# Two-layer graph network with mixture of experts: edge work re-paced, all first-layer output products ahead of the table, table's zeros moved up

## The chip, the cores and the metric

The kernel runs on one core of a Trainium2 chip. The metric is device time in microseconds (us), lower is better: the median of 3 runs of the kernel before is 2243.9 us (2240.32 to 2245.11).

## The reference, cut to what matters

625 nodes with 1024 features, 10,000 edges. Layer 0 adds a graph attention and a linear attention to x, then a feed-forward block with ternary weights; layer 1 follows with a mean over neighbours, another linear attention, and experts. The change touches layer 0 and the start of layer 1:

```python
xn = _layernorm(x)
# graph attention (4 heads of 64)
h = rmsnorm(xn) @ W_down;  xl = h @ Wl;  xr = h @ Wr
e = (leaky_relu(xl[src] + xr[dst]) * att).sum per head
alpha = segment_softmax(e, dst);  gat = segment_sum(alpha * xl[src], dst) @ W_up
# linear attention (16 heads)
q, k = elu(xn @ W + b) + 1;  v = xn @ W_v + b_v
kv = k^T v per head;  mix = (q kv / (q sum(k) + eps)) @ W_o + b_o
x = x + gat + mix
x = x + ffn(_layernorm(x))        # weights rounded to -1, 0, 1 by their mean size
xn = _layernorm(x)                # layer 1: k and v products of its attention come first
```

Self loops are added to the edges. The softmax needs no order of edges: scores are exponentiated and written into a dense table by (source, destination), and repeated edges are handled by a matrix of counts.

## The kernel before, in words

Nodes are in 5 tiles of 125 rows. Five engines work side by side, each in program order: TensorE (products), VectorE and ScalarE (elementwise), GpSimd (indirect transfers), SyncE (SP; weight loads). Inside layer 0 the order on each engine is the order in which the Python code emits instructions.

**Stream.** `do(prep, pe, after, after2)` emits the products `pe` of one step; its `after` (evictions by VectorE and ScalarE) is emitted at the next call of `do`, `after2` at the one after that. So an eviction stands on VectorE behind whatever was emitted for the step in between.

**Edge stage (L378 to L723).** The 10,000 edges are 79 chunks of 128 (the last of 16), two chunks to a group, 40 groups. For a chunk GpSimd gathers the rows xl[src] and xr[dst] (L588, two indirect transfers); VectorE adds them, applies `att` and sums to scores (L596, L568, L569, L571); ScalarE exponentiates (L575); GpSimd scatters the scores into a table of 128 × 3080 rows of 4 in DRAM (L602). The table is filled with zeros first (L554, one 6.16 MB transfer of SP, put behind the first loads of Wk, Wv and their biases). The tiles `ga`, `gb` have 4 buffers each.

Meanwhile TensorE does layer 0's linear attention: for each of two halves of the features, 5 key and 5 value pieces (L241, L261: 8 products of 512 columns each), after each of which 6 chunks of edges are counted (L436: 5 products each from one-hot rows that VectorE makes); then the states kv; then 8 queries and answers (L302, L322), in which VectorE takes reciprocals (L333); then the output products `mixed(t)` (L691: for each half of the output 8 products of 512 columns). `mixed(0)` is begun in this stage, the other tiles' come later.

**What paces the edges.** Each piece of TensorE calls `work(us)` with a cost written in by hand: 6.9 for a key or value, 0.7 for a counted chunk, 3.0 for a state, 8.5 for a query, 3.5 for an answer. Whenever these units pass the next multiple of 7.6, one beat is emitted (L642): scores of group g−2, exponentials of group g−3, and for each of the two chunks two gathers of group g and one scatter of group g−3. In beats 1 to 5 the self loops of a tile are added (L618). Beats that are left over are emitted after the last step (L720).

**After the table (L725 to L1038).** `load_table(t)` reads the block of one tile of destinations back (L760, GpSimd's queue); x is loaded again on the same queue (L972). Here too the absolute sums of the three feed-forward weights are taken (L736), their mean is made by a small product (L740), and the weights are rounded (L751). `weigh(t)` multiplies the table's block by the counts (L774, VectorE). The loop over p (L992 to L1034) then does for tile p `sums` (pg, L797), `turn_sums`, and `up_again` (L829), whose product is accumulated into the same PSUM tile as `mixed(p)`; and for tile p−1 the feed-forward block (f1 to f4), for tile p−2 the second normalisation (p5, f5). Biases `bo` are added to x at L1020, two tiles in each of p = 0, 1 and the last in p = 2. Two slots in each turn of p hold a `spacer` (L982): one half of `mixed(p+2)` while p+2 < 5, and from p = 3 on a key or value piece of layer 1; what is left of those follows the loop (L1035). Layer 1's weights are loaded at p = 3 (L995).

Of the kernel before, what the change touches and what calls it, by code (L numbers as in the profile page):

```python
# [53 lines left out]
def attempt(ctx: ExitStack, tc: tile.TileContext, w: dict, out: bass.AP, shifted: bool):  # L54
# [161 lines left out]
    class LinearAttention:  # L216
# [13 lines left out]
        def half(self, c):  # L230
            Wk, bk, Wv, bv = (w[n] for n in self.names[1:])
            self.wk, self.wv = Half(wpool, Wk, c), Half(wpool, Wv, c)
            self.bk, self.bv = self.bias(bk, c, "bk_t"), self.bias(bv, c, "bv_t")
            self.kf = mid([P, NT, 512], "kf")
            self.v = mid([P, NT, 4, 129], "v")
            nc.gpsimd.memset(self.v[:, :, :, 128:129], 1.0)
            self.kv.append(mix.tile([128, 4, 256], FP, tag="kv", name="kv", bufs=2))

        def key(self, t):
# [19 lines left out]
            self.work(6.9)  # L259

        def value(self, t):  # L261
# [12 lines left out]
            self.work(6.9)  # L274

        def states(self):
# [5 lines left out]
            def state(a):  # L282
# [15 lines left out]
                self.work(3.0)  # L298
# [3 lines left out]
        def query(self, m):  # L302
# [17 lines left out]
            self.work(8.5)  # L320

        def answer(self, m, oT):  # L322
# [14 lines left out]
            self.work(3.5)  # L337

    with ExitStack() as st0:
# [8 lines left out]
        with ExitStack() as edges:  # L348
# [31 lines left out]
            nc.gpsimd.memset(none, FAR if shifted else 0.0)  # L380
            sf = pool.tile([128, EN], FP, name="sf")
# [153 lines left out]
            for t in range(NT):  # L535
# [9 lines left out]
                if t == NT - 2:  # L545
# [8 lines left out]
            nc.sync.dma_start(out=table.rearrange("(p a b) h -> p a (b h)", p=128, a=28),  # L554
                              in_=none.unsqueeze(1).to_broadcast([128, 28, 440]))

# [25 lines left out]
            def gather(g, j):  # L582
                lo, n, p = groups[g]
                if j == 0:
                    ab[g] = [pool.tile([128, G, 256], FP, tag=k, name=k, bufs=4) for k in ("ga", "gb")]
                if j < n:
                    for dst, src, ix in ((ab[g][0], xl_d, si), (ab[g][1], xr_d, di)):
                        nc.gpsimd.indirect_dma_start(  # L588
                            out=dst[0:p, j, :], out_offset=None, in_=src[:, :],
                            in_offset=bass.IndirectOffsetOnAxis(ap=ix[0:p, lo + j:lo + j + 1], axis=0))  # L590
# [8 lines left out]
            def scatter(g, j):  # L599
                lo, n, p = groups[g]  # L600
                if j < n:
# [38 lines left out]
            beat = dict(us=0.0, g=0)  # L640

            def work(us):  # L642
                beat["us"] += us
                while beat["us"] >= 7.6 * beat["g"] and beat["g"] < len(groups) + 3:
                    g = beat["g"]
                    beat["g"] += 1
                    if 1 <= g <= NT:
                        self_loops(g - 1)
                    if g >= 3:
                        lo, n, p = groups[g - 3]  # L650
                        exp(es[0:p, lo:lo + n, :])
                    if 2 <= g < len(groups) + 2:
                        score_group(g - 2)
                    for j in range(G):
                        if g < len(groups):
                            gather(g, j)
                        if g >= 3:
                            scatter(g - 3, j)
# [3 lines left out]
            for c in range(2):  # L662
                if c:
                    lin.half(c)
                for t in range(NT):
                    for f in (lin.key, lin.value):
                        f(t)
                        part["held"] = max(part["held"] - 1, 0)
                        for _ in range(6):
                            if count():  # L670
                                work(0.7)
# [19 lines left out]
            def mixed(t, ks=range(KC)):  # L691
                for c in range(2):
                    def pe(c=c):
                        if c == 0 and ks[0] == 0:
                            hold["px", t] = ps2("px1")
                        for k in ks:
                            nc.tensor.matmul(hold["px", t][:P, c, :], lhsT=oT[:, k, nodes(t)], rhs=wo[c](k),  # L697
                                             start=(k == 0), stop=False)

                    yield lambda pe=pe: do(None, pe)  # L700

            for m in range(KC):
                if m + 1 < KC:
                    lin.query(m + 1)
                else:
                    for f in mixed(0, range(6)):
                        f()
# [10 lines left out]
            bo = [lin.bias(w["L0_bo"], c, tag) for c, tag in enumerate(("bk_t", "bv_t"))]  # L718
            do.flush()
            while beat["g"] < len(groups) + 3:  # L720
                work(8.0)
# [6 lines left out]

        gu = wpool.tile([128, KC, 512], BF, tag="w", name="gu", padded_shape=[128, KC, 512])
        dn = late.tile([128, 2, D], BF, name="dn")  # L730
        made = [gu[:, :, 0:256], gu[:, :, 256:512], dn]
        part3 = late.tile([128, 3], FP, name="part3")
        wmean = late.tile([128, 3], FP, name="wmean")
        wscale = late.tile([128, 3], FP, name="wscale")

        def weight_sums():  # L736
            for i in range(3):
                nc.vector.tensor_reduce(part3[:, i:i + 1], raw[i], AX.X, ALU.add, apply_absolute_value=True)

        def weight_means():  # L740
            def pe():
                hold["pm"] = ps1("pm")
                group(hold["pm"][:, 0:3], [(ones, part3)])

            def after():
                nc.vector.tensor_scalar(wmean, hold["pm"][:, 0:3], 1.0 / (256 * D), 1e-5, op0=ALU.mult, op1=ALU.max)
                nc.vector.reciprocal(wscale, wmean)

            do(None, pe, after)

        def ternary(i):  # L751
            v = raw[i]
            nc.vector.tensor_scalar(v, v, wscale[:, i:i + 1], 1.0, op0=ALU.mult, op1=ALU.min)
            nc.vector.tensor_scalar(v, v, -1.0, MAGIC, op0=ALU.max, op1=ALU.add)
            m = made[i]
            nc.vector.tensor_scalar(m, v.rearrange("p (k n) -> p k n", k=m.shape[1]), MAGIC, None,
                                    op0=ALU.subtract)
# [71 lines left out]
        def up_again(t):  # L829
            px = hold.pop(("px", t))  # L830
# [1067 lines left out]
```

## Time and profile before

| what | value |
|---|---|
| median of 3 runs | 2243.9 us |
| profiled execution: its own time | 2243.64 us |
| profiled execution: span | 2241.8 us |
| TensorE busy | 2126.3 us (95%) |
| VectorE / ScalarE / GpSimd busy | 713.6 / 194.7 / 347.6 us |
| TensorE busy, 150 to 200 us, granted clock | 35.5 of 50 us, 0.85 |
| TensorE busy, 250 to 300 us, granted clock | 35.4 of 50 us, 0.86 |
| TensorE busy, 300 to 350 us, granted clock | 39.8 of 50 us, 0.89 |
| TensorE busy, 550 to 600 us, granted clock | 40.6 of 50 us, 0.90 |
| TensorE busy, 650 to 700 us, granted clock | 50.0 of 50 us, 1.00 |

The span is that of the instructions on the chip; the execution's own time lies 1.84 us above it. "Busy" counts an engine's instructions only; a waiting engine is idle. A product in 32-bit floats appears as two matrix instructions in the profile, so a piece of 8 products is listed as x16. The granted clock is TensorE's rate as a share of full speed. In a timeline each row has start, duration, engine, line, operation, output and inputs, how many, and in brackets the idle time before it with what ended it.

### The profile page before, as it was taken

The numbers are of one execution on the slowest core, as the hardware profiler recorded it, in microseconds if no ns is written. First come the engines' busy times: TensorE is split into PE (matmuls) and PEld (weight loads), VectorE is DVE, ScalarE is ACT, GpSimd is POOL, SyncE is SP. The second block draws the span as 40 slices with busy tenths as digits, with TensorE's granted clock in tenths as the row PEclk, the third lists the DMA queues.
The fourth block names the chain that finished last, engine by engine and source line by source line (L and its number), as shares of the span: only waits on it lengthen the run. The fifth ranks groups of instructions, "written<-read, shape, count | busy, mean of one in ns | idle before, by whom it ended". The sixth has DMA issues, their size and how long they took to land. (4 is left out here: it accounts for less than half of the span.)

```text
span 2241.8 us, 17353 instructions
## 1 busy us (share of the span) xinstructions
PE 2126.3 (95%) x6934; PEld 1217.0 (54%) x6934; DVE 713.6 (32%) x1212; ACT 194.7 (9%) x354; POOL 347.6 (16%) x351
## 2 busy tenths in 40 slices
PE   7988788898899989999999999999999999999998
PEld 6655365454444657764445767556754444444443
DVE  4864556766421580000113124322111111111112
ACT  2100011011110210000000111110000000000000
POOL 1676767300000040010000000110000000000010
PEclk9999899998899999999999999999999999999999
DMA  9334253421122110231212111030198997898742
GB/s 286 114 108 136 67 175 102 113 83 47 38 85 75 41 54 1 75 141 38 75 38 103 38 38 38 19 103 29 65 334 320 332 330 279 325 332 296 267 148 93
DMA packets 145849, 301.63 MB, mean 135 GB/s; under 512 B 12370, under 2 KB 22436, under 8 KB 145754
## 3 DMA queue, kind: packets, MB, share of 16 engines
q1 hardware_dynamic: 123412, 243.18, 30.5%
q0 software_dynamic: 17664, 47.47, 7.1%
q10 hardware_dynamic: 4678, 9.72, 1.4%
q8 instruction: 58, 0.95, 0.2%
q14 instruction: 37, 0.30, 0.0%
HBM read 277.49 MB, written 22.84 MB: 134 GB/s over the span
## 5 line engine op out<-in xcount | busy, mean ns | idle before, releaser
L130 PE MATMUL pu<-w,xgT 128*128 128x512 f32 x768 | 333.9, 593 | 1.9 <-DVE xgT L1192 1.9
L130 PEld LDWEIGHTS pu<-w,xgT 128*128 128x128 f32 x768 | 144.0, 190 | 174.8 <-issue 172.0
L130 PE MATMUL pyb<-w,hb 128*128 128x512 f32 x384 | 174.3, 598 | 2.4 <-ACT yb L105 2.1
L130 PE MATMUL pq<-xnT,w 128*128 128x313 f32 x512 | 144.1, 441 | 16.1 <-DVE v L269 14.6
L130 PE MATMUL pk<-w,xnT 128*125 128x512 f32 x320 | 141.0, 593 | 4.7 <-DVE x L940 4.7
L130 PE MATMUL pv<-w,xnT 128*125 128x512 f32 x320 | 140.7, 592 | 1.2 <-ACT xnT L956 1.2
L130 PE MATMUL p<-tT,w 128*128 128x313 f32 x512 | 136.3, 428 | 0.4 <-DVE tT L1192 0.4
L130 PEld LDWEIGHTS pq<-xnT,w 128*128 128x128 f32 x512 | 100.3, 197 | 59.3 <-DVE v L269 15.4
L130 PEld LDWEIGHTS pyb<-w,hb 128*128 128x128 f32 x384 | 69.8, 189 | 90.9 <-issue 74.8
L130 PEld LDWEIGHTS p<-tT,w 128*128 128x128 f32 x512 | 96.8, 190 | 37.9 <-issue 1.2
L1732 DVE TENSOR_TENSOR su<-pu,su 128x512 f32<-128x512 f32 x24 | 16.6, 692 | 314.6 <-ACT su L1731 314.6
L130 PEld LDWEIGHTS pk<-w,xnT 128*125 128x125 f32 x320 | 59.4, 188 | 78.1 <-issue 71.2
L130 PEld LDWEIGHTS pv<-w,xnT 128*125 128x125 f32 x320 | 59.7, 188 | 73.3 <-issue 71.6
L1715 POOL DMA_INDIRECT xg<-rows_d,slots x12 | 11.4, 949 | 524.7 <-PE pxg L1722 448.9
L602 POOL DMA_INDIRECT table<-es,at x79 | 82.7, 1047 | 56.6 <-issue 25.5
L588 POOL DMA_INDIRECT ga<-xl_d,si x79 | 81.7, 1034 | 32.5 <-issue 21.7
L588 POOL DMA_INDIRECT gb<-xr_d,di x79 | 82.3, 1042 | 24.1 <-issue 23.8
L697 PE MATMUL px<-w,oT 128*125 128x512 f32 x160 | 75.0, 625 | 6.3 <-DVE oT L334 4.6
L130 PE MATMUL px<-w,hT 128*125 128x512 f32 x160 | 70.3, 592 | 0.0
L130 PE MATMUL px<-w,oT 128*125 128x512 f32 x160 | 70.3, 592 | 0.0
L130 PE MATMUL ph<-meanT,w 128*128 128x313 f32 x256 | 70.1, 426 | 0.0
L130 PE MATMUL ph<-xnT,w 128*128 128x313 f32 x256 | 70.0, 427 | 0.0
(365 smaller groups left out, 2476.5 us busy)
## 6 DMA issues: line engine op xcount, KB each, us to landing
w<-in_eW_dram SPq DMA_DIRECT2D x144, 1024.0 KB
w<-in_L_Wk_dram SPq DMA_DIRECT2D x8, 1024.0 KB
w<-in_L_Wv_dram SPq DMA_DIRECT2D x8, 1024.0 KB
w<-in_L_Wq_dram SPq DMA_DIRECT2D x8, 1024.0 KB
w<-in_L_Wo_dram SPq DMA_DIRECT2D x8, 1024.0 KB
w<-in_W_self_dram SPq DMA_DIRECT2D x8, 1024.0 KB
w<-in_W_neigh_dram SPq DMA_DIRECT2D x8, 1024.0 KB
w<-in_sW_dram SPq DMA_DIRECT2D x8, 1024.0 KB
```

Source lines behind the costliest of these rows:

```text
L130: nc.tensor.matmul(dst, lhsT=lhsT, rhs=rhs, start=(i == 0), stop=(i == len(pairs) - 1))
L588: nc.gpsimd.indirect_dma_start(out=dst[0:p, j, :], out_offset=None, in_=src[:, :], in_offset=bass.IndirectOffsetOnAxis(ap=ix[0:p, lo + j:l ...
L602: nc.gpsimd.indirect_dma_start(out=table[:, :], out_offset=bass.IndirectOffsetOnAxis(ap=at[0:p, lo + j:lo + j + 1], axis=0), in_=es[0:p, l ...
L697: nc.tensor.matmul(hold["px", t][:P, c, :], lhsT=oT[:, k, nodes(t)], rhs=wo[c](k), start=(k == 0), stop=False)
L1715: nc.gpsimd.indirect_dma_start(out=xg, out_offset=None, in_=rows_d[:, :], in_offset=bass.IndirectOffsetOnAxis(ap=slots[:, b:b + 1], axis=0))
L1732: nc.vector.tensor_tensor(su, pu[:, 0, :], su, op=ALU.mult)
```

## The change

- *Pacing.* The units become 4.8 for a key or value, 0.72 for a counted chunk, 0.6 for a state, 8.6 for a query, 2.7 for an answer, 0.6 per product of `mixed`; a beat is 8.2 units. Scores lag 3 groups, exponentials 4, scatters 5; from the output products on, 1, 1 and 2. Scatters are taken from one list of chunks, up to two in a beat, up to four in a beat with short lags.
- *Output products.* All five tiles' `mixed` are emitted in the edge stage. The PSUM tiles of 0, 1 and 2 stay as before; those of 3 and 4 are evicted with the bias added into an SBUF tile `kept`, and are added to x in place of the bias. `up_again` for these two starts a new PSUM tile. The weight sums, means and rounding move into the edge stage as well, between the output products.
- *Loop.* No spacers at p = 0 and 1; one (the second) at p = 2; both from p = 3 on. All spacers are key and value pieces of layer 1. The biases of tiles 0 and 1 are added at p = 0, the rest at p = 1. Layer 1's first weights are loaded at p = 0. The second `load_table` stands behind all loads of x.
- *Zeros.* The 6.16 MB transfer is issued right behind the loads of x, W_down, Wl and Wr.

```diff
-            self.work(6.9)
+            self.work(4.8)
-                self.work(3.0)
+                self.work(0.6)
-            self.work(8.5)
+            self.work(8.6)
-            self.work(3.5)
+            self.work(2.7)
...
             nc.gpsimd.memset(none, FAR if shifted else 0.0)
+            nc.sync.dma_start(out=table.rearrange("(p a b) h -> p a (b h)", p=128, a=28),
+                              in_=none.unsqueeze(1).to_broadcast([128, 28, 440]))
...
             lin.half(0)
-            nc.sync.dma_start(out=table.rearrange("(p a b) h -> p a (b h)", p=128, a=28),
-                              in_=none.unsqueeze(1).to_broadcast([128, 28, 440]))
...
+            chunks = [(g, j) for g, (lo, n, p) in enumerate(groups) for j in range(n)]
+            def scatter(last):
+                if chunks and chunks[0][0] <= last:
+                    g, j = chunks.pop(0)
...
+            lags = [3, 4, 5]
+            def one_beat():
+                g = beat["g"]
+                beat["g"] += 1
+                if 1 <= g <= NT:
+                    self_loops(g - 1)
+                if lags[1] > lags[0]:
+                    raise_all(g - lags[1])
+                    scores(g - lags[0])
+                else:
+                    scores(g - lags[0])
+                    raise_all(g - lags[1])
+                for j in range(G):
+                    if g < len(groups):
+                        gather(g, j, 0)
+                        if lags[1] == lags[0]:
+                            scatter(g - lags[2])
+                        gather(g, j, 1)
+                    scatter(g - lags[2])
             def work(us):
                 beat["us"] += us
-                while beat["us"] >= 7.6 * beat["g"] and beat["g"] < len(groups) + 3:
...
+                while beat["us"] >= 8.2 * beat["g"] and chunks:
+                    one_beat()
...
-                                work(0.7)
+                                work(0.72)
...
+            lags[:] = 1, 1, 2
+            kept = mid([P, 2, 2, 512], "kept")
+            mixed(3, keep=kept[:, 0])
+            weight_sums()
+            mixed(4, keep=kept[:, 1])
+            weight_means()
+            mixed(0, range(6, KC))
+            for t in (1, 2):
+                mixed(t)
+                ternary(t)
+            ternary(0)
             do.flush()
-            while beat["g"] < len(groups) + 3:
-                work(8.0)
+            while chunks:
+                one_beat()
...
         load_table(0)
-        weight_sums()
-        for f in mixed(0, range(6, KC)):
-            f()
-        weight_means()
-        do()
-        for i in range(3):
-            ternary(i)
         for t in range(NT):
             rows_dma(nc.gpsimd, x[:, t, :], xrows[t])
-            if t == 0:
-                load_table(1)
-        first_mixed = list(mixed(1))
-        first_mixed[0]()
+        load_table(1)
         weigh(0)
-        first_mixed[1]()
...
-        def spacer(p, c):
-            if p + 2 < NT:
-                if c == 0:
-                    made_of["mixed"] = list(mixed(p + 2))
-                made_of["mixed"][c]()
-            else:
-                f, t = next(kv_pieces)
-                getattr(lin1, f)(t)
+        def spacer():
+            f, t = next(kv_pieces)
+            getattr(lin1, f)(t)
         for p in range(NT + 2):
             do()
-            if p == NT - 2:
-                lin1.half(0)
...
-            spacer(p, 0)
+            if p >= 3:
+                spacer()
...
-            for t in range(2 * p, min(2 * p + 2, NT)):
+            for t in ((0, 1), (2, 3, 4))[p] if p < 2 else ():
                 for c in range(2):
                     xc = x[:, t, c * 512:(c + 1) * 512]
-                    nc.vector.tensor_tensor(xc, xc, bo[c][:P], op=ALU.add)
-            if p <= NT:
-                spacer(p, 1)
+                    nc.vector.tensor_tensor(xc, xc, bo[c][:P] if t < 3 else kept[:, t - 3, c, :], op=ALU.add)
+            if p == 0:
+                lin1.weights(0)
+            if p == 1:
+                lin1.half(0, loaded=True)
+            if 2 <= p <= NT:
+                spacer()
```

`scores(last)` and `raise_all(last)` emit the scores and exponentials of all groups up to `last` that are not emitted yet.

## Prediction

> **What bounds the kernel now.** I read the page first: over the 2241.8 us span TensorE is busy 2126 us, and the slices that are not full lie in the first third.
>
> ```profile
> PE   7988788898899989999999999999999999999998
> PEclk9999899998899999999999999999999999999999
> ```
>
> Each digit is 56 us; the diff touches only slices up to about 650 us. From 624 us on the timeline shows TensorE without a gap for a long way, so a change is worth what it moves that point. Next the waits of TensorE and VectorE before 850 us (total us, times, longest):
>
> ```profile
> PE po L130 <- DVE oT L334: 18.6, 11, 3.7
> PE pq L130 <- DVE v L269: 14.6, 1, 14.6
> PE pkv L130 <- DVE v L269: 8.8, 1, 8.8
> DVE ga L596 <- DMA gb<-xr_d,di: 105.6, 27, 8.4
> ```
>
> TensorE waits for VectorE, and VectorE sits with a score at its head (L596) that waits for a gather. So GpSimd's edge transfers are behind. Its timeline (start, us) says why they end when they do:
>
> ```profile
> 59.83 1.27 POOL L588 DMA_INDIRECT ga<-xl_d,si  x1 [8.41 <-DMA table<-none]
> 203.95 1.00 POOL L602 DMA_INDIRECT table<-es,at  x1 [0.30 <-issue]
> 268.79 1.00 POOL L602 DMA_INDIRECT table<-es,at  x1 [0.30 <-issue]
> 393.39 1.47 POOL L602 DMA_INDIRECT table<-es,at  x1 [2.85 <-DMA table<-es,at]
> 396.26 0.97 POOL L602 DMA_INDIRECT table<-es,at  x1 [1.40 <-DMA table<-es,at]
> 399.13 0.96 POOL L602 DMA_INDIRECT table<-es,at  x1 [1.91 <-DMA table<-es,at]
> 410.81 0.85 POOL L602 DMA_INDIRECT table<-es,at  x1 [1.91 <-issue]
> 413.43 0.90 POOL L164 DMA_DIRECT2D tb<-table  x1 [1.76 <-DMA table<-es,at]
> ```
>
> From 59.8 us GpSimd issues nearly back to back: between the rows at 203.95 and 268.79 lie 48 transfers, 1.35 us each. There are 237 (79 chunks, three each), some 322 us of issuing. The last scatters, with no gathers between, come 2.87 us apart. The table is read from 413.43. Then the handover, on TensorE and VectorE:
>
> ```profile
> 419.47 19.28 PE L697 MATMUL px<-w,oT 128*125 128x512 f32 x43
> 428.14 4.91 DVE L774 TENSOR_TENSOR pT<-tb,CT 125x500 f32<-125x500 f32 x5
> 438.59 4.48 PE L130 MATMUL pg<-xl,pT 125*125 125x65 f32 x40
> 455.67 1.29 DVE L857 BATCH_NORM_STATS2 st<-x 125x6 f32<-125x512 f32 x2
> 485.02 1.27 DVE L857 BATCH_NORM_STATS2 st<-x 125x6 f32<-125x512 f32 x2
> 513.94 1.28 DVE L857 BATCH_NORM_STATS2 st<-x 125x6 f32<-125x512 f32 x2
> 524.72 8.66 PE L130 MATMUL pg<-xl,pT 125*125 125x65 f32 x40 [0.93 <-ACT xnT L956]
> 552.18 1.27 DVE L857 BATCH_NORM_STATS2 st<-x 125x6 f32<-125x512 f32 x2
> ```
>
> While the table is on its way TensorE does output products (L697); its first sum (pg) starts at 438.59. The statistics of one node tile after another (L857) then come 29.4, 28.9 and 38.2 us apart. That is the loop's period, a chain through VectorE and TensorE.
>
> [...] the 40 pg products take 4.48 us in a busy stretch and 8.66 us at 524.72 after short gaps. [...] here a scatter lands 2.1 us after its issue, and a scatter waits for the scatter before it. [...]
>
> **The change, part by part.** All against the profiled execution (span 2241.8, its own time 2243.64, 0.26 under the median of 2243.9). A difference of 0.2%, 4.5 us, is about what a measurement tells from no change.
>
> *A, zeros.* They (6.16 MB) move in SP's queue from behind to ahead of the first key and value weights (4 MB) and two biases. In the built order of the changed program the first half of Wk also waits for the semaphore lane that the zeros use. The loads ahead are some 4.1 MB, moved by about 19.5 us (132 to 284 GB/s in the 5 us stretches); the zeros at about 340 GB/s take 18.5 more, landing near 40; [...] Wk at about 46, and TensorE asks for it at 48.14. Behind that wait on SP stand the other three halves and both biases; they follow 3 us apart, and TensorE and VectorE ask for them later than that. Cost +1 (0 to +5). The first gather may start a few us before 59.83: worth nothing, since from now the pacing holds GpSimd.
>
> *B, when the table is done.* A key or value piece takes TensorE 6.87 us (timeline, 69.87 to 76.74) but now counts 4.8; six counts take 4.00 us for 4.32. A beat of 8.2 thus takes 10.87 × 8.2 / 9.12 = 9.8 us, and without counts 6.87 × 8.2 / 4.8 = 11.7. Before it was 7.6 / 11.1 × 10.87 = 7.4 us, under the 8.2 that GpSimd needs for six transfers, hence the stalls. Now VectorE waits less and GpSimd idles. With four gather buffers a gather waits for the score four groups back, one beat earlier. Without stalls query 0 starts at 48.1 + 20 × 6.87 + 79 × 0.667 + 4 × 1.12 = 242.7, when 155.3 units have passed: beats 0 to 18, beat 19 with that query. GpSimd has then issued 80 gathers and, scatters starting at beat 5, 30 scatters by about 246: 110, where before had 129. The other 127 × 1.36 = 172.7 bring it to 418.9. Added: 4 because in the query part scores stand behind VectorE's 5.7 us of reciprocal and its neighbours; 2 for the catching-up beats, in which scatters alternate with single gathers (2.72 us against the 2.87 that one needs); 4.5 for the last three scatters; 1.8 to the read. So the read is at 431.2 instead of 413.4: +17.8 (+10 to +25; high if the 4 MB of next weights, now loaded as soon as the output products are done, slow scatters as the stalls at 297 to 312 suggest).
>
> The stalls removed from TensorE (8.8, 14.6, most of 18.6, half clock after them) don't count: TensorE is done near 404 and waits for the table.
>
> *C, handover.* Before, 438.59 − 413.43 = 25.2 us. The ternary weights (L753 to L756, 11.3 us) and output products that stood in it are now done ahead of it. Left: 0.9 second issue, 7.5 landing, 4.9 weighing, 0.2: 13.5. −11.7.
>
> *D, tile 0.* TensorE has been idle some 35 us: pg takes up to 8.7 instead of 4.5. The four bias adds stay. Before, 17.0 from pg to x; now 8.7 + 0.8 + 0.8 + 7 (up product at half rate) + 1.2 = 18.5 to 19.5. +2 (0 to +4).
>
> *E, tile 1.* Two product pieces (13.7 us) leave, but VectorE's chain remains: statistics to xq 6.7, transposes to hidden 7.7, weighing 4.95, bias adds (now six) 3.6, tail 4: about 28 with waits, before 29.4. −1 (−4 to +1).
>
> *F, tile 2.* Two product pieces leave, one key comes, in the second slot. That is the row of tile 3 (38.2) without its first slot (pg starts 5.8 earlier), but with a key where it had a value: its bias add (0.7) and its Exp and Relu on ScalarE (1.36 us, VectorE's wait between L248 and L256) now stand ahead of the copy of goT that the up product waits for, so that product starts some 3.5 after the piece instead of 1.1 (544.64 to 545.76): +2.4. 34.8 against 28.9: +6 (−4 to +8).
>
> *G, tiles 3 to 5.* Keys and values change slots: +2.4, and −1.1 for pg's wait behind the same ScalarE work at 524.72 and 562.97 (0.93 and 1.15), each; the last without an up product. +3 (−2 to +6).
>
> *H.* One key or value piece fewer is left after the loop: −6.9.
>
> Free: four evictions of kept tiles (4 × 0.69) and 6.7 us of weight sums on VectorE, hidden under 13.7 us product pieces with no eviction of their own; uncovered they would cost 9.5. The second table read, now behind ten loads of x on GpSimd's queue (0.5 to 1.3 each), lands near 450, and the weighing that needs it comes after the half-rate pg, near 454; were pg at full rate, up to 2 of D would go there.
>
> Sum: 1 + 17.8 − 11.7 + 2 − 1 + 6 + 3 − 6.9 = +10.2, so 2254.
>
> **Rivals.** *The loop was held by TensorE (faster).* Place: tiles 1 and 2. For: in 462.66 to 491.76 TensorE is busy 27.4 of 29.1 us, VectorE 20.4. Then the removed pieces shorten tiles 1 and 2 by 4 each and the slot exchange costs nothing: E and F −4, G 0: 1 + 17.8 − 11.7 + 2 − 8 − 6.9 = −5.8, 2238. It decides once the distance of the statistics in tile 2 falls under 25 us. Against: most of VectorE's other 8.7 us are waits inside the chain itself, for products that wait for VectorE.
>
> *Transfers collide (slower still).* A at +5 and B at +25: 2265. For: GpSimd's stalls at 297 to 312 fall on weight loads issued from 292.5.
>
> *It cancels.* B at +11 with F near zero: 2240 to 2248. For: before also had some 10 us of scatter stalls that might not recur.
>
> **How the numbers follow.** Forecast 0.52 at 2254 (2249 to 2262); TensorE-held loop 0.17 at 2238; collisions 0.17 at 2265; cancelling 0.14. Faster 0.17, same 0.14, slower 0.69. The range 2236 to 2266 leaves about half of the first and third rival's cases out.
>
> **What would show it.** Right: TensorE without waits over 2 us from 48 to 400, then idle some 35 us; first table read near 431; sums at half clock; L857's successor about 28, then 35 us apart. Wrong: the table read before 420; TensorE waiting for Wk at 48; tile 2 under 29 us; or waits inside the edge stage that I count as gone.

## The result and the profile after

The changed kernel takes 2252.94 us (median of 13 runs, 2248.77 to 2262.26), the kernel before beside it 2240.59 us (13 runs, 2237.92 to 2245.11): a ratio of 1.0052, 95% interval 1.0042 to 1.0062, so some 12 us slower. The profiled execution has a span of 2251.8 us and its own time is 2253.51 us, 9.9 above that of before.

The page of the changed kernel has these rows of 40 slices, 56 us each:

```profile
PE   7999999158899989999999999999999999999998
PEclk9999999668999999999999999999999999999999
```

TensorE's waits between 56 and 394 us are gone from the first row (slices 1 to 6, counted from 0, are full, where before they read 988788), and one hole has come in their place, at 400 to 460 us, with a lower clock in and behind it (the two sixes). The waits of TensorE and VectorE before 850 us, of the changed kernel (total us, times, longest), give its name:

```profile
PE pg L130 <- DVE pT L817: 55.4, 6, 53.8
PE po L130 <- DVE oT L338: 6.1, 7, 2.7
DVE ga L599 <- DMA gb<-xr_d,di: 43.5, 9, 10.1
```

VectorE's waits for gathers fell from 105.6 to 43.5 us and TensorE's for the answers from 18.6 to 6.1 (all 6.1 of them lie behind 760 us, in layer 1); pg, the first sum over the table, waits 53.8 us. GpSimd's timeline shows why (start, us), first one row of before, then the changed kernel:

```profile
220.46 1.00 POOL L602 DMA_INDIRECT table<-es,at  x1 [0.30 <-issue]
```

```profile
246.68 0.96 POOL L591 DMA_INDIRECT ga<-xl_d,si  x1 [6.23 <-DVE es L574]
...
439.04 0.97 POOL L609 DMA_INDIRECT table<-es,at  x1 [1.91 <-ACT es L578]
441.40 0.96 POOL L609 DMA_INDIRECT table<-es,at  x1 [1.40 <-DMA table<-es,at]
444.27 0.85 POOL L609 DMA_INDIRECT table<-es,at  x1 [1.91 <-issue]
446.78 0.89 POOL L164 DMA_DIRECT2D tb<-table  x1 [1.66 <-issue]
```

The rows at 220.46 and 246.68 are each the 111th of 237 edge transfers; in the changed kernel it is held back 6.23 us by VectorE's score (es). The table is read from 446.78, 33.4 us later than before. TensorE is done with all output products at 402.45 and stands still, as its timeline shows:

```profile
371.31 31.14 PE L723 MATMUL px<-w,oT 128*125 128x512 f32 x72
456.29 0.68 PE L130 MATMUL pg<-xl,pT 125*125 125x65 f32 x2 [53.84 <-DVE pT L817]
```

And VectorE's: the weighing ends its wait for the table, then come the statistics of the first three node tiles (L902 here, L857 before):

```profile
455.20 4.83 DVE L817 TENSOR_TENSOR pT<-tb,CT 125x500 f32<-125x500 f32 x5 [15.99 <-DMA tb<-table]
...
470.71 4.89 DVE L817 TENSOR_TENSOR pT<-tb,CT 125x500 f32<-125x500 f32 x5 [2.77 <-DMA tb<-table]
...
479.23 1.29 DVE L902 BATCH_NORM_STATS2 st<-x 125x6 f32<-125x512 f32 x2
505.38 1.28 DVE L902 BATCH_NORM_STATS2 st<-x 125x6 f32<-125x512 f32 x2
542.02 1.27 DVE L902 BATCH_NORM_STATS2 st<-x 125x6 f32<-125x512 f32 x2
```

The second weighing (470.71), that of tile 1, stands on VectorE ahead of tile 0's statistics and waits for the second read of the table. The statistics are 26.2 and 36.6 us apart, before 29.4 and 28.9. A mark behind all of it is pkv, layer 1's first state product: 652.09 before, 663.38 after, 11.3 later. From there to the end the two take 1589.7 and 1588.4 us. In every run below this last part lies between 1586.5 and 1591.0; what differs lies ahead of pkv, so each run is read as two numbers: when the table is read, and how long from there to pkv.

| | table read | read to pkv | pkv |
|---|---|---|---|
| before | 413.43 | 238.7 | 652.09 |
| after | 446.78 | 216.6 | 663.38 |

The change loses 33.4 us before the read and gets 22.1 back after it.

One thing must be known to read the experiments. They ran on three chips (numbers 9, 0 and 13) on which the kernel before takes 2281 to 2288 us, and the same edge stage comes to the table's read 22 to 39 us later than in this comparison. Which chip this comparison ran on is not known, so whether it is the chip that differs is not shown. Each ratio has the kernel before on the same chip beside it; it is not exactly the quotient of the two medians. A read time comes from one profiled execution per kernel, while the executions of one kernel spread over 17 us or more, so a few us between two reads can be chance.

### The profile page after: what moved, and what is told of

Its sections match the earlier page's. It is cut to its first block, busy times and chain, and to the rows that moved or that the text cites. A ratio compares the mean times of both kernels' runs of the same rounds, so it can differ in the third digit from the quotient of the medians.

```text
span 2251.8 us, 17353 instructions
## 1 busy us (share of the span) xinstructions
PE 2115.4 (94%) x6934; PEld 1211.3 (54%) x6934; DVE 715.1 (32%) x1216; ACT 194.6 (9%) x354; POOL 341.6 (15%) x351
## 5 line engine op out<-in xcount | busy, mean ns | idle before, releaser
L130 PE MATMUL pq<-xnT,w 128*128 128x313 f32 x512 | 138.1, 428 | 2.0 <-ACT qf L319 1.2
L591 POOL DMA_INDIRECT ga<-xl_d,si x79 | 79.9, 1012 | 62.7 <-DVE es L574 22.9
L130 PE MATMUL pg<-xl,pT 125*125 125x65 f32 x200 | 32.2, 332 | 57.5 <-DVE pT L817 55.4
L130 PE MATMUL px<-w,oT 128*125 128x512 f32 x160 | 70.3, 592 | 0.0
```

The costliest lines, as they stand in the source:

```text
L130: nc.tensor.matmul(dst, lhsT=lhsT, rhs=rhs, start=(i == 0), stop=(i == len(pairs) - 1))
L591: nc.gpsimd.indirect_dma_start(out=ab[g][side][0:p, j, :], out_offset=None, in_=src[:, :], in_offset=bass.IndirectOffsetOnAxis(ap=ix[0:p, ...
```

## The experiments

**Before with the zeros moved (part A alone).**

```diff
             nc.gpsimd.memset(none, FAR if shifted else 0.0)
+            nc.sync.dma_start(out=table.rearrange(...), in_=none...)
...
             lin.half(0)
-            nc.sync.dma_start(out=table.rearrange(...), in_=none...)
```

> The kernel before with one part of the change alone: the table's zeros are written right behind the loads of x. The theory (the zeros are harmless where they stand now) expects the first pk of layer 0 no more than 1 us later, the first gather about 3.5 us earlier (59.8 to about 56.3, as in the changed kernel), and the time at -2 us against before, between -3.5 and +1, as GpSimd is the queue that sets the end of the edge stage there. The rival (the zeros' 10 us in front of the weights on SP delay the whole stage) expects +3 to +10 us.

Measured: 2288.27 us beside 2287.84 for before, ratio 0.9999 (0.9977 to 1.0020): −0.2 us, between −5.3 and +4.6. The first gather starts at 53.97; the run below, which has the zeros where before has them, starts it at 61.29 on the same chip, and its first pk at 49.77, against 45.30 here. The rival's +3 to +10 is nearly shut out; a gain of 2 and none can't be told apart.

**Before with the pieces of layer 1 exchanged (part of G alone).**

```diff
-        kv_pieces = iter([(f, t) for t in range(NT) for f in ("key", "value")])
+        kv_pieces = iter([(f, t) for t in range(NT) for f in ("value", "key")])
```

> The kernel before with layer 1's pieces in the loop taken as value, key, value, key instead of key, value: in each tile the piece ahead of pg is then one whose output VectorE takes and ScalarE does not touch, as in the changed kernel. The theory (the loop's gain of 10 us over the tiles with pieces comes from this exchange, since a key piece's exp on ScalarE holds back the copy that pg and its neighbours wait for) expects pg of those tiles at 4.6 us instead of 7.6 to 8.7, tile periods of 38 us down to about 34, and the time at -8 us against before (-5 to -11). The rival (the loop is bound by VectorE's own chain, and the gain came from the products that were taken out of the loop) expects 0, at most 2 us to either side.

Measured: 2281.32 us beside 2287.84, ratio 0.9965 (0.9945 to 0.9985): −8.0 us (the medians are 6.5 apart), as the theory had it; the rival's 0 is outside, its −2 too. The timeline of TensorE, first of the run with the zeros moved (same chip, pieces in the order of before), then of this one:

```profile
552.90 7.13 PE L130 MATMUL pk<-w,xnT 128*125 128x512 f32 x16 [1.43 <-DVE x L939]
564.21 8.66 PE L130 MATMUL pg<-xl,pT 125*125 125x65 f32 x40 [0.77 <-ACT xnT L955]
...
591.07 7.13 PE L130 MATMUL pk<-w,xnT 128*125 128x512 f32 x16 [1.44 <-DVE x L939]
...
691.46 4.94 PE L130 MATMUL pkv<-v,kf 125*128 125x129 f32 x40
```

```profile
563.77 7.13 PE L130 MATMUL pv<-w,xnT 128*125 128x512 f32 x16 [1.43 <-DVE x L940]
573.34 4.58 PE L130 MATMUL pg<-xl,pT 125*125 125x65 f32 x40 [0.68 <-ACT xnT L956]
...
597.78 7.13 PE L130 MATMUL pv<-w,xnT 128*125 128x512 f32 x16 [1.43 <-DVE x L940]
...
692.42 4.94 PE L130 MATMUL pkv<-v,kf 125*128 125x129 f32 x40
```

With a key ahead of it pg starts 11.31 us after the start of the piece and takes 8.66; with a value ahead of it 9.57 and 4.58. A tile takes 34.0 us instead of 38.2, and from the first piece to pkv it is 128.65 instead of 138.56: −9.9.

**After with the pieces exchanged back.** The same edit in the changed kernel: its third round now takes a value in its second slot, and from then on keys stand in front of pg.

> The changed kernel with layer 1's pieces in the loop taken as value, key, value, key, so that from the fourth round of the loop on the piece ahead of pg is a key again, as in the kernel before. All else of the change stays. The theory of the exchange expects the periods of these tiles to go from 33 or 34 us back to about 37 or 38, and the time +8 us against the changed kernel (+5 to +11), some 1.009 of before. The rival (the gain is from the products taken out of the loop) expects the changed kernel's 1.005 of before, within 2 us.

Measured: 2283.79 us, ratio 0.9987 (0.9971 to 1.0004). The tile periods come back as expected, in TensorE's timeline of this run:

```profile
560.82 7.13 PE L130 MATMUL pk<-w,xnT 128*125 128x512 f32 x16 [1.43 <-DVE x L985]
...
598.19 7.13 PE L130 MATMUL pk<-w,xnT 128*125 128x512 f32 x16 [1.44 <-DVE x L985]
...
636.37 7.13 PE L130 MATMUL pk<-w,xnT 128*125 128x512 f32 x16 [1.44 <-DVE x L985]
```

37.4 and 38.2, in place of 34.0 and 32.9. Not all of it is lost: in the third round the value lets the next piece start 13.9 us after it (546.88 to 560.82), where a key takes 17.5 (549.36 to 566.89 in the next run), so 3.6 come back. Read to pkv is 224.0 against 219.2 in the next run, +4.8, little more than half of what I expected. The ratio expected, 1.009, did not come. In part that is because the changed kernel itself does not stand at 1.005, as the next run shows. But at its 0.9984 (on another chip) the 8 us, 0.0035 of the time, don't show in the ratios either: the price of the exchange in the changed kernel is seen in the trace and not in the time.

**After as it is, again.**

> The changed kernel as it stands, once more, beside the runs it is to be compared with. In the first runs of this study, on a chip on which the kernel before took 2288 us instead of 2241, the changed kernel with its slots exchanged came to 0.9987 of before, where the first comparison and the exchange's price of 8 us had led to expect 1.009. If the change's effect is the same everywhere, this gives 1.005 (1.004 to 1.006). If the edge stage of before suffers more on some chips than that of the changed kernel, it gives 0.995 on such a chip and 1.005 on one like the first.

Measured: 2278.45 us beside 2281.11, ratio 0.9984 (0.9967 to 1.0001). It is level with before, not 0.5% behind. The table is read at 469.57, pkv is at 688.80. On these chips engines stand still in the edge stage where the profile shows nothing that holds them. An example from TensorE's timeline, near 132 us, in the first profile of the changed kernel and then in this one:

```profile
131.93 4.16 PE L447 MATMUL pct<-ring 128*125 128x313 bf16 x30
```

```profile
132.12 0.34 PE L447 MATMUL pct<-ring 128*125 128x313 bf16 x1 [0.34 <-issue]
134.23 0.43 PE L447 MATMUL pct<-ring 128*125 128x313 bf16 x2 [1.76 <-issue]
134.97 0.32 PE L447 MATMUL pct<-ring 128*125 128x313 bf16 x1 [0.32 <-issue]
136.35 0.42 PE L447 MATMUL pct<-ring 128*125 128x313 bf16 x1 [1.07 <-issue]
```

Thirty products in 4.16 us there; here they come one or two at a time, with gaps put down to "issue" (no releaser seen). TensorE's gaps of that kind (and the few marked "remote") between 48 and 480 us come to 0 in both first profiles and to 10 to 51 us in all twelve of these (a later expectation gives 40 to 95 us for each engine; for TensorE that is too much in most of them). Here TensorE ends its products at 430.9 instead of 402.45, and it costs nothing beyond the table's own delay of 23 us: it still waits 48.5 us in front of pg. The kernel before has no such reserve; in the run with the zeros moved, which takes the same time as before, the read is 28 us later than in the first profile of before and read to pkv 11 us longer. That reserve is my reading of why the change's loss vanishes there. It is not tried by itself, and what stops the engines stays open.

**After with the key and value pieces charged at what they take**, run on two chips.

```diff
-            self.work(4.8)
+            self.work(6.9)
...
-            self.work(4.8)
+            self.work(6.9)
```

> The changed kernel with the key and value pieces of layer 0 charged at 6.9 instead of 4.8 us (what the trace shows that one of them takes at TensorE: 6.87 us), all else kept: 20 pieces times 2.1 us is 42 us of charge that lets gathers out earlier. The theory (the pace holds GpSimd back early in the stage, and the late table comes from that) expects GpSimd without the pauses of up to 10 us between 50 and 250 us, the first read of the table issued 10 to 25 us earlier than at 446.8, and the time -15 us against the changed kernel (-8 to -25), that is at or below the kernel before. The rival (the table is late because of short waits of single transfers and of the shared queues in the last 60 us) expects less than 4 us of gain; a second rival (VectorE is then stopped by gathers that have not landed, and TensorE behind it) a loss of up to 10 us.

> The changed kernel with the key and value pieces of layer 0 charged at 6.9 instead of 4.8 us, once more. On the chips of the earlier runs each engine stood still for 40 to 95 us of the edge stage with nothing in the profile that held it, which drowns a difference of this size; if this chip is like the first one, where that was under 3 us, the theory (beats of 10.9 x 8.2 / 11.2 = 8.0 us in the key and value part instead of 9.8) expects GpSimd's 110th transfer near 230 instead of 247, the read near 432 instead of 447, and the time 1.000 of before (0.996 to 1.002) instead of 1.005. The rival (the four buffers with a lag of 3 hold GpSimd, whatever the charge) expects the 110th transfer later than 240 and 1.003 to 1.005.

Measured: 2283.74 us, 0.9981 (0.9963 to 0.9998), and 2280.24 us, 0.9990 (0.9973 to 1.0007). The charge moves GpSimd the way the theory says: its 111th transfer starts at 250.6 and 244.4 instead of 263.6, and the table is read at 464.75 and 458.42 instead of 469.57. On one and the same chip the gain is smaller: the run with the pieces exchanged back has the changed kernel's edge stage, was on the chip of the first of these two, and reads at 468.45, 3.7 us later. And the time does not follow. TensorE's timeline, second run:

```profile
437.04 31.14 PE L723 MATMUL px<-w,oT 128*125 128x512 f32 x72
470.04 0.43 PE L130 MATMUL pg<-xl,pT 125*125 125x65 f32 x2 [1.85 <-DVE pT L817]
```

Its products end at 468.2 instead of 430.9, and the 48.5 us of waiting in front of pg are now 1.85. TensorE's other waits before the table went from 19.7 to 46.3 us; 30.8 of these are gaps without a releaser (17.9 in the changed kernel's run), so what slows it is seen only in part. It is not the second rival's way: VectorE does not wait for a gather in either run.

Yet pg starts at 470.04 here and at 479.38 in the changed kernel's run, 9.3 us earlier, while pkv comes only 1.4 earlier. Most of the gain is lost behind pg, and VectorE's timeline shows the first place, in the changed kernel's run and in this one:

```profile
495.60 4.86 DVE L817 TENSOR_TENSOR pT<-tb,CT 125x500 f32<-125x500 f32 x5 [4.57 <-DMA tb<-table]
```

```profile
491.65 4.84 DVE L817 TENSOR_TENSOR pT<-tb,CT 125x500 f32<-125x500 f32 x5 [9.96 <-DMA tb<-table]
```

The second weighing waits for the second read of the table, and tile 0's statistics follow 8.5 us after its start in both. The 4 MB of layer 1's first weights are issued at 457.91 here, 0.5 us before the first read of the table (458.42), so I take them to be under way during the reads; in the changed kernel's run they were issued at 420.65. The last run of "Both together" bears on this.

**After with scores two beats behind their gathers**, also twice.

```diff
-            lags = [3, 4, 5]
+            lags = [2, 3, 4]
```

> The changed kernel with the lags of the edge stage set to 2, 3, 4 instead of 3, 4, 5 (scores two beats behind their gathers, as in the kernel before), the pace kept. There are four buffers for gathered rows: with a lag of 3 a gather waits for the score of the beat just before, so GpSimd can be no more than one beat ahead of VectorE; with a lag of 2 it can be two beats ahead. The theory (the beat's length alone holds GpSimd) expects it to be one beat ahead once and for all: the table's read 8 us earlier (5 to 10), time -8 us against the changed kernel. The rival (the buffers hold it: GpSimd's waits for VectorE's es, 36.8 us in the changed kernel, go) expects the read 15 to 25 us earlier and time -15 to -25. A third possibility: VectorE then waits for gathers that have not landed, and nothing is won.

> The changed kernel with lags 2, 3, 4 instead of 3, 4, 5, once more. If this chip is like the first one: the theory (the beat alone holds GpSimd, the lag gives it one beat once) expects the 110th transfer 8 to 10 us earlier than 247, the read near 438, and the time 1.001 of before (0.999 to 1.003). The rival (the buffers hold it) expects the read 15 to 25 us earlier and 0.995 to 0.998. The opposite is possible too: an earlier run had the read 12 us later with these lags, because VectorE then stood longer in front of gathers or single stalls fell differently; that would be 1.006 or more.

Measured: 2286.77 us, 1.0018 (0.9999 to 1.0038), and 2285.06 us, 1.0007 (0.9989 to 1.0025). The first is slower than the changed kernel on the same chip (2278.45 us, 0.9984). Both theories missed: the 111th transfer is at 263.0 and 262.8, hardly earlier than 263.6, and the read at 481.64 and 479.66, 10 to 12 later. GpSimd's waits in the first of them (total us, times, longest):

```profile
POOL table L609 <- ACT es L578: 29.8, 8, 8.0
POOL table L609 <- issue: 28.5, 61, 3.6
POOL ga L591 <- DVE es L574: 24.3, 6, 13.5
...
POOL table L609 <- DMA table<-own: 19.5, 1, 19.5
```

The gathers' waits for a score did fall (over their two lines from 67.3 us in the changed kernel's run to 36.2), and more came back at the scatters: they wait for the score's exponential (29.8, in the changed kernel's run 1.9), which stands one beat ahead of them as it did, and once for the self loops' own rows (19.5), which they now follow a beat earlier. So GpSimd stands for VectorE's scores at one place or the other; that this is why the read does not come earlier is my reading of these waits.

**Both together**, twice, the second time with layer 1's first weights moved as below.

> The changed kernel with lags 2, 3, 4 and the key and value pieces of layer 0 charged at 6.9 instead of 4.8 us. Charging alone, in an earlier run, moved the table's read by only some 4 us against the run beside it, with 66 us of GpSimd's waits for VectorE's es left. The theory (pace and buffers hold GpSimd together, and each alone leaves the other) expects those waits under 10 us, the read 20 to 30 us earlier than the changed kernel's on the same chip, and time -20 us against it (-12 to -28). The rival (the tail's short waits make the table late) expects less than 8 us. A second rival (VectorE, held by gathers, stops TensorE as in the kernel before) expects the read early but TensorE's edge stage ending 10 to 20 us later, so -5 to -10.

> The changed kernel with both: lags 2, 3, 4 and 6.9 us for the key and value pieces. If this chip is like the first one: with pace and buffers as free as in the kernel before, the 110th transfer near 222 as there (220.5), the read at 415 to 425, TensorE at the end of its output products at 405 to 420, and the loop as in the changed kernel: 0.992 of before (0.988 to 0.996). If VectorE's waits for gathers stop TensorE as in the kernel before (33 us there), TensorE ends its products near 435 and the gain is some 10 us only against the changed kernel: 1.000 of before. On a chip with the stalls that the profile does not show, 0.998 as in the earlier run of it.

> The run before (lags 2, 3, 4; 6.9 us) and layer 1's first key and value weights on GpSimd's queue behind the table's reads. The theory of the collision expects the stretch of the last 40 transfers 2 to 4 us shorter than without that, and time -3 us against that run (-1 to -6). The rival (no resource shared that matters, or the weights wait elsewhere already) expects 0, within 2 us. It is also the version with the most of the table's delay taken out: if the mechanisms hold, it is faster than both kernels.

Measured: 2276.06 us, 0.9982 (0.9967 to 0.9996); 2276.79 us, 0.9985 (0.9968 to 1.0003); with the weights moved 2274.84 us, 0.9966 (0.9951 to 0.9980). Reads at 455.99, 460.64 and 470.73. With the lags 2, 3, 4 the charge does pay: both together are 10.7 and 8.3 us under the lags alone on the same chip, by the medians. But they are no faster than the changed kernel as it is (0.9984), though the read is 9 to 14 us earlier than in its run; pkv is at 679.42 and 691.64 around its 688.80. The third ratio is, with the exchange in the kernel before (0.9965), the lowest of all. That it is better than its neighbour's 0.9985 or the changed kernel's 0.9984 is not shown, as the intervals overlap, and its profiled execution (2284.19 us) is the slowest of its 22, so its late read says little.

What the weights do, its trace does show. Times in us; the last column goes from the first read to tile 0's statistics:

| run | weights issued | second read issued | second weighing starts | read to statistics |
|---|---|---|---|---|
| changed kernel again | 420.65 | 483.11 | 495.60 | 34.5 |
| charge alone, second | 457.91 | 474.95 | 491.65 | 41.7 |
| both, second | 466.81 | 475.08 | 492.66 | 40.5 |
| both, weights moved | 493.44 | 484.09 | 495.64 | 33.4 |

In the four runs with the charge and the weights on SP's queue the second weighing starts 16.3 to 17.6 us after the second read is issued; in the seven other runs of the changed kernel's kind it is 11.1 to 12.5. The last two rows differ in the weights' place alone, and 7 us from read to statistics go with it. So there is a collision, but with the table's second read and not with the last scatters, which it was to test: those were over at 457.1, before SP issued the weights.

**After with layer 1's first weights behind the table's reads.**

```diff
-                nc.sync.dma_start(out=t, in_=v[:, 4 * i:4 * i + 4, c * 512:(c + 1) * 512])
+                (on or nc.sync).dma_start(out=t, in_=v[:, 4 * i:4 * i + 4, c * 512:(c + 1) * 512])
...
-            self.wk, self.wv = (Half(wpool, w[self.names[i]], c) for i in (1, 3))
+            self.wk, self.wv = (Half(wpool, w[self.names[i]], c, on=None if c else self.rows_on) for i in (1, 3))
```

> The changed kernel with layer 1's first key and value weights (4 MB) issued on GpSimd's queue behind the reads of the table, instead of on SP's, where they start at 392 us, while the last 30 or so edge transfers are still to come; they are asked for only at about 513. Scatters and single issues between 381 and 414 us took 0.6 to 1.2 us longer than elsewhere there. The theory of the collision (those weights slow the last scatters and gathers) expects the read of the table 4 to 8 us earlier and time -6 us against the changed kernel. The rival (they share no resource that matters) expects the read within 2 us of the changed kernel's and time 0 to +2, the latter if the weights then come late for the first value piece of the loop.

Measured: 2275.39 us, 0.9986 (0.9966 to 1.0006), against 0.9984 for the changed kernel on the same chip. SP's queue in the changed kernel (first profile) and GpSimd's in this run:

```profile
392.18 3.81 SPq L121 DMA_DIRECT2D w<-in_L_Wk_dram  x2
399.05 3.80 SPq L121 DMA_DIRECT2D w<-in_L_Wv_dram  x2
```

```profile
485.35 1.56 POOL L121 DMA_DIRECT2D w<-in_L_Wk_dram  x2
486.87 1.52 POOL L121 DMA_DIRECT2D w<-in_L_Wv_dram  x2
```

From the 191st to the last edge transfer this run takes 73.1 us, the unchanged one beside it 76.2. That would be 3 us of collision, under the 4 to 8 expected; but the run with the pieces exchanged back, with the weights on SP's queue at 425 us, takes 73.6, so even the 3 are not shown. The read came 6.3 earlier, half of that from before this stretch. In the time nothing is seen.

## Why the prediction was right, and which steps were not

The total (2254 forecast, 2252.94 measured; +10.2 on the way to pkv against +11.3) is right, but two of its terms, B and G, are 13 to 16 us wrong and cancel, and so do two smaller ones, C and D, at 4 us each. That the sum came out so close is luck. The path was right: TensorE, done with its products at 402.45 (forecast near 404), stands and waits for the table, and its saved stalls are worth nothing there.

- **A, zeros: +1 forecast, at most +0.9 seen.** The first pk moved from 48.14 to 49.00 with no wait for its weights; their issue on SP waited 10.0 us for the zeros, until 41.53. Moved alone they give −0.2 (−5.3 to +4.6).
- **B, table read: +17.8 forecast, +33.4 measured, outside its own range.** The part up to the 111th transfer holds: 110 transfers "by about 246", and the 111th came at 246.68, though it had waited 6.2 us for a score. The rest failed in the term "the other 127 × 1.36 = 172.7" with 12.3 added. That is 185.0 us from the 111th transfer to the read; the kernel before itself took 413.43 − 220.46 = 193.0 for it, and the changed one takes 200.1. Without the 4 us that the sum has for waits on scores it is 181.0, so 12 of the 15 us of error are a stretch priced below what it took before: 1.36 us is the rate of its best part, while before took 1.43 a transfer up to the 191st and 1.65 behind it. The waits on scores came as priced (4.4 up to the 191st), and scatters there waited 2.4 us longer for scatters. The changed kernel does not catch up: 26.2 us behind at the 111th, 32.6 at the 191st, 33.5 at the last. The last 46 transfers cost only 0.9 more than before (76.9 against 76.0), so the alternating scatters are no visible gain or loss. A collision with weights there, priced at the top of the range, is not shown (at most 3).
- **The cause of B, pacing, is right in direction and half a story.** Charging the pieces at their measured time brings the read forward, by 3.7 us on one chip and by 5 and 11 across chips, far less than 33. It does not bring the time: TensorE's products end later, and the second read of the table then waits behind layer 1's weights.
- **C and D, handover and tile 0: −9.7 forecast, −9.8 measured, by luck.** Read to statistics is 42.24 before and 32.45 after. The handover C was 9.5 instead of 13.5, since pg's first products start as soon as the first slice is weighed (at 456.29, 1.09 us after the weighing's start at 455.20): −15.7 for −11.7. Tile 0, D, was 22.9 instead of 18.5 to 19.5, +5.9 for +2, outside its range: pg at a granted clock of 0.50 takes 10.8 for 8.7, and VectorE waits 2.8 us for the second read, which the prediction had under "Free".
- **E, tile 1: −1 forecast, −3.2. F, tile 2: +6 forecast, +7.7**, and the up product starts late after the key as said: 3.0 us behind the piece's end.
- **G, tiles 3 to 5: +3 forecast, −10.1 measured, wrong sign.** Three tiles took 38.2, 37.4 and 25.8 us before and 34.0, 32.9 and 24.4 after. The prediction priced two effects of the exchange: +2.4 for the key's exp ahead of goT's copy, and −1.1 for pg's wait. Both are there (px waits 1.16 for goT at 569.51; pg's wait went from 0.93 and 1.15 to 0.68). The missing one is TensorE's clock: of the 4.2 us that the first of these tiles gains, pg itself gives 4.1 and the short products behind it 1.1, the earlier start of pg 1.7, and the later up product takes 2.6 back. The three windows below are the piece, the stretch between it and pg, and pg, first of before and then of after (us, busy time and instructions of each engine, granted clock, DMA share, GB/s):

```profile
513.00:520.60 7.60, 7.18 (x18) 3.27 (x19) 6.70 (x14) 1.87 (x3) 0.00 (x0) 1.00 0.00 0
520.60:524.70 4.10, 1.25 (x8) 0.63 (x6) 2.64 (x6) 1.77 (x4) 0.00 (x0) 0.82 0.00 0
524.70:533.40 8.70, 8.68 (x42) 8.68 (x43) 0.22 (x1) 0.45 (x1) 0.00 (x0) 0.50 0.01 2
```

```profile
541.50:548.60 7.10, 7.10 (x18) 3.19 (x19) 6.20 (x13) 0.59 (x2) 0.00 (x0) 1.00 0.01 2
548.60:551.00 2.40, 1.10 (x9) 0.64 (x7) 2.23 (x5) 1.17 (x2) 0.00 (x0) 1.00 0.00 0
551.00:555.60 4.60, 4.54 (x42) 4.54 (x43) 0.00 (x0) 0.01 (x1) 0.00 (x0) 1.00 0.00 0
```

With a key ahead, the stretch is 4.1 us and TensorE busy for 1.25 of it, since the key's own evictions stand in front of the copies it waits for (ScalarE 1.77 us); the granted clock is 0.82 over that stretch and 0.50 for the whole of pg. With a value ahead it is 2.4 us, and here the clock stays at 1.00. But 2.4 is no safe gap. In the second run with the charge, pg starts 9.57 us after the start of the value in two tiles in a row:

```profile
560.36 7.13 PE L130 MATMUL pv<-w,xnT 128*125 128x512 f32 x16 [1.43 <-DVE x L985]
569.93 7.93 PE L130 MATMUL pg<-xl,pT 125*125 125x65 f32 x40 [0.68 <-ACT xnT L1001]
...
598.18 7.13 PE L130 MATMUL pv<-w,xnT 128*125 128x512 f32 x16 [1.43 <-DVE x L985]
607.74 4.58 PE L130 MATMUL pg<-xl,pT 125*125 125x65 f32 x40 [0.68 <-ACT xnT L1001]
```

In six of the traces (the changed kernel's first, the exchange in the kernel before, and the four runs on chip 13) twelve such sums start between 550 and 620 us: 8 take 4.58 us and 4 take 7.83 to 8.01; behind a key (before, zeros moved, pieces exchanged back) all 6 take 7.22 to 8.66. So with a value ahead the short time is possible but not certain; what parts the 8 cases from the 4 is not shown. In the second run of "Both together" both sums are slow (7.83 and 8.01 us), and the three tiles take 99.3 us, where the changed kernel took 91.3 and before 101.4. So some 8 of the 10.1 us go with how long these sums take. The prediction even quotes 8.66 as its example for this row, but then treats it as a constant of the row when the piece ahead is exchanged. The exchange alone in the kernel before is worth −8.0 us (−12.6 to −3.4).
- **H, one piece fewer: −6.9 forecast, −6.7** (from the last tile's piece to pkv 37.3 and 30.6).

Of the rivals, "the loop was held by TensorE" gave the tiles 1 and 2 −4 each; tile 1 came near it, and tile 2 at 36.6 is far over its 25. "Transfers collide" came nearer to B with its +25, but its reason is not shown. "It cancels" is what the other chips show, by another way: there, if my reading holds, the reserve of TensorE in front of the table takes up what would else be lost.

## What to carry to other kernels

Price a stretch that has waits in it by what the kernel before took for that same stretch, not by the rate of its best part. When a stage has two queues that finish close together, look at both ends before one is paced by the other's cost, and at what comes next: a read that was free may be the next wait. And where a short product stands behind a gap, price the two together: pg took 8.66 us behind a stretch of 4.1 us and 4.58 behind one of 2.4. A reordering that shortens the gap may halve such a product, though not in every run (7.83 to 8.01 in 4 of 12 cases).

## What the runs showed that was not expected

- The order of two equal pieces in a loop (a key or a value first, 7.13 us each) is worth 8 us in 2288, much of it by the duration of the sum behind them: the same 40 products in 4.58 or 8.66 us (in the traces of the comparison at a granted clock of 1.00 or 0.50). With the same 9.57 us from the start of the piece ahead, the same sum still takes 4.58 or 7.93.
- On the chips of the experiments the same programs take 25 to 47 us more, and all of it lies ahead of pkv. There TensorE's gaps without a releaser sum to 10 to 51 us between 48 and 480 us, where the first profiles have none, and a change that cost 0.52% is level. The reads of one kernel on two chips lie 2 to 6 us apart (481.64 and 479.66; 464.75 and 458.42; 455.99 and 460.64).
